# Second layer of a two-layer vision network: the recurrence's product gets an SBUF tile of its own, and a later input stands between product and sum

## The chip, the cores and the metric

The kernel runs on one core of one Trainium2 chip. The metric is the device time of one execution in microseconds (us). The version before the change has a median of 8306.25 us over three runs (8298.19 to 8308.66).

## What is computed

The network has two layers on an image batch of 16 x 128 x 56 x 56 in float32. The first layer (routed window attention with a feed-forward part) is not touched by the change. The second layer is a 3x3 convolution, whose output is read as many short sequences of 8 tokens with 16 channels, each of which goes through a small selective state-space model (32 inner channels, 16 states each), followed by a group normalisation and a residual sum. What matters here is the recurrence over the 8 tokens:

```
dA = jnp.exp(dt[..., None] * A)
dBx = dt[..., None] * Bm[:, :, None, :] * xc[..., None]
def step(h, inp):
    a, b, c = inp
    h = a * h + b
    return (h, jnp.sum(h * c[:, None, :], axis=-1))
```

Each token multiplies the state by its decay `a`, adds the input `b`, and weighs the new state with `c`.

## The kernel before, in words

**Layout.** The two layers run one after the other. The second one (function `layer1`) works through 16 images x 7 blocks = 112 groups. A group is 448 sequences in the free dimension. For one token its state has 32 x 16 = 512 values for each sequence, held as an SBUF tile `h` of 128 x 4 x 448; a token is done in two halves (`jp` 0 and 1) of 128 x 2 x 448 = 128 x 896 elements, so that 7 tokens to be advanced in two halves make 14 steps `k` of a group.

**What one token needs.** TensorE spreads the step sizes times the decay rates into a PSUM tile `a` (`decay`, L973; two buffers), and ScalarE takes the exponential in place (`decay_exp`, L976). TensorE spreads the inputs into a PSUM tile `x` (`spread`, L984; one buffer), and VectorE multiplies it with the token's row of `B` (tile `bb`, brought by DMA) into the SBUF tile `h`: this is the token's input (`inject`, L991). VectorE then makes the product of decay and previous state, in place in PSUM (`advance`, L1001), and adds it to the input (`complete`, L1006). The last token (l = 7) leaves out the sum: its product goes straight to `h` (L999), since its input reaches the output by another way (`product`, `direct`, `direct_mul`). GpSimd multiplies the whole state of a token, 128 x 1792 elements, with the token's row of `C` (`weigh`, L1010), and TensorE sums over the states (`gather`, L1019). `collect` (L1032) adds the direct part, tile `ud`; `gated` (L1035) is on GpSimd.

**Order of work.** The order on each engine is written out by hand in the loop at the end of `layer1`, and `_chain` keeps every engine to it; each engine works through its own queue in that order. At step k of a group VectorE gets `advance` of step k, what `work` puts in its list (`collect`, statistics), `complete` of step k, and `inject` for step k + 4; at k = 0 the list (`direct_mul`) comes after the `inject`. TensorE then gets `decay` for step k + 2 and `spread` for step k + 5, and ScalarE the exponential. At every odd k GpSimd gets `weigh` for the token just finished, and then the list of the step. GpSimd's queue in a group is therefore: weigh 1 (k = 1), in some groups a part of the store (k = 2, L1126), weigh 2 (k = 3), the second `gated` of the previous group (k = 4), weigh 3 (k = 5), four operations of `rate_sum` for the next group (k = 6, L922 to L925), weigh 4 (k = 7), four more (k = 8), weigh 5 (k = 9), `product` (k = 10, L951), weigh 6 (k = 11), weigh 7 (k = 13), the first `gated`.

**Buffers.** `h` has four buffers, given out in the order of the code: tokens 0 to 6 when their input is made, token 7 when its product is made. So the `inject` at k = 12, for token 1 of the next group, takes the buffer of token 5, which is free when weigh 5 is done; the one at the next k = 0 takes that of token 6 and waits for weigh 6. `w1` to `w4` are SBUF pools with one to four buffers for each tag.

The first layer has one line that matters as a comparison: `position` (L303), a multiply-add on VectorE that reads two SBUF tensors, runs beside the GpSimd operations of `beside` (L313 and L315), which work on other tiles.

The loop that sets the order:

```
if now:
    advance(*state_step(i, k))
for part in dve if k else ():
    part()
if now:
    complete(*state_step(i, k))
if inputs:
    inject(*inputs)
```

Of the kernel before, what the change touches and what calls it, by code (L numbers as in the profile page):

```python
# [10 lines left out]
F32 = mybir.dt.float32  # L11
U32 = mybir.dt.uint32
AF = mybir.ActivationFunctionType
ALU = mybir.AluOpType
# [3 lines left out]
P = 128  # L18
# [5 lines left out]
BLK = 448  # L24
# [771 lines left out]
def layer1(ctx: ExitStack, tc: tile.TileContext, x1, t, out, conv):  # L796
# [15 lines left out]
    nc = tc.nc  # L812
# [3 lines left out]
    cst = ctx.enter_context(tc.tile_pool(name="l1c", bufs=1))  # L816
    w1 = ctx.enter_context(tc.tile_pool(name="l1w1", bufs=1))
    w2 = ctx.enter_context(tc.tile_pool(name="l1w2", bufs=2))
# [14 lines left out]
    vec = conv.vec  # L833
# [5 lines left out]


    for w, name in ((wx, "b_kx"), (wv, "b_dtw")):
        k = w1.tile(list(w.shape), F32, tag="fold", name=name)
        nc.sync.dma_start(k, t[name])
        nc.vector.tensor_mul(w, w, k)
    nc.scalar.activation(adec, adec, AF.Exp)
    nc.vector.scalar_tensor_tensor(adec, adec, -1.0, mask, ALU.mult, ALU.mult)
    dd = cst.tile([P, P], F32, tag="dd", name="dd")
    nc.vector.tensor_scalar_mul(dd, ident, d_w)
    eps = cst.tile([P, 1], F32, tag="eps1", name="eps1")
    nc.vector.memset(eps, GN_EPS)  # L850
    neg = cst.tile([P, 1], F32, tag="neg", name="neg")
    nc.vector.memset(neg, -1.0)

    y, tails = conv.y, conv.tails
    pq = [ps_q.tile([P, 512], F32, tag=f"q{k}", name=f"pq{k}") for k in range(2)]
# [11 lines left out]
    def own(jp):  # L867
        return slice(2 * jp, 2 * jp + 2)
# [86 lines left out]
        nc.tensor.matmul(pq[0][:, 0:BLK], lhsT=cbm, rhs=p["cb"], start=True, stop=True)  # L955

    def direct_mul(p):
        ud = p["ud"] = w2.tile([P, 2, BLK], F32, tag="ud", name=f"ud_{p['n']}")
        for h in range(2):
            nc.vector.scalar_tensor_tensor(  # L960
                ud[:, h, :], pq[0][:, 0:BLK], vec[:, 6 + h : 7 + h], p["dtx"][:, h, :], ALU.mult, ALU.mult
            )


# [3 lines left out]
    def decay(p, l, jp):  # L968
        h, l4 = divmod(l, 4)
        a = p["a", l, jp] = ps_a.tile([P, 2, 512], F32, tag="a", name=f"a_{p['n']}_{l}_{jp}")[:, :, 0:BLK]  # L970
        for k in range(2):
            rows = slice(32 * (2 * jp + k), 32 * (2 * jp + k) + 32)
            nc.tensor.matmul(a[:, k, :], lhsT=adec[rows, l4, :], rhs=p["dt"][rows, h, :], start=True, stop=True)  # L973

    def decay_exp(p, l, jp):
        nc.scalar.activation(p["a", l, jp], p["a", l, jp], AF.Exp)  # L976

    def spread(p, l, jp):

        h, l4 = divmod(l, 4)  # L980
        x = ps_x.tile([P, 2, 512], F32, tag="x", name=f"x_{p['n']}_{l}_{jp}")[:, :, 0:BLK]
        for k in range(2):
            rows = slice(32 * (2 * jp + k), 32 * (2 * jp + k) + 32)
            nc.tensor.matmul(x[:, k, :], lhsT=mask[rows, l4, :], rhs=p["dtx"][rows, h, :], start=True, stop=True)  # L984
        px["x"] = x

    def inject(p, l, jp):
        if jp == 0:
            p["h", l] = w4.tile([P, 4, BLK], F32, tag="h", name=f"h_{p['n']}_{l}")
        weight = p["gate", 0, l].unsqueeze(1).to_broadcast([P, 2, BLK])  # L990
        nc.vector.tensor_mul(p["h", l][:, own(jp), :], px["x"], weight)  # L991

    def advance(p, l, jp):

        a, before = p["a", l, jp], p["h", l - 1][:, own(jp), :]
        if l == 7:
            if jp == 0:
                p["h", l] = w4.tile([P, 4, BLK], F32, tag="h", name=f"h_{p['n']}_{l}")
            nc.vector.tensor_mul(p["h", l][:, own(jp), :], a, before)  # L999
        else:  # L1000
            nc.vector.tensor_mul(a, a, before)  # L1001

    def complete(p, l, jp):
        if l < 7:
            h = p["h", l][:, own(jp), :]
            nc.vector.tensor_add(h, p["a", l, jp], h)  # L1006

    def weigh(p, l):
        c = p["c", l] = w4.tile([P, 4, BLK], F32, tag="cst", name=f"cst_{p['n']}_{l}")
        nc.gpsimd.tensor_mul(c, p["h", l], p["gate", 1, l].unsqueeze(1).to_broadcast([P, 4, BLK]))  # L1010
# [18 lines left out]
    def collect(p, h):  # L1029
        if h == 0:  # L1030
            p["ym"] = w1.tile([P, 2, BLK], F32, tag="ym", name=f"ym_{p['n']}")
        nc.vector.tensor_add(p["ym"][:, h, :], pq[1][:, 0:BLK], p["ud"][:, h, :])  # L1032

    def gated(p, h):
        nc.gpsimd.tensor_mul(p["ym"][:, h, :], p["ym"][:, h, :], p["zs"][:, h, :])  # L1035
# [117 lines left out]
    def work(i, k):  # L1153
# [8 lines left out]
        if prev:  # L1162
            if k == 0:
                pe += [partial(gather, prev, 5), partial(gather, prev, 6)]
            if k == 1:
                pe.append(partial(gather, prev, 7))
            if k == 3:
                dve.append(partial(collect, prev, 1))
            if k == 4:
                pool.append(partial(gated, prev, 1))  # L1170
            if k in (5, 6):
                pe.append(partial(project_out, prev, k - 5))
            b = prev["b"]
            if prev["g"] % 2 and k in (9, 10):
                dve.append(partial(statistics, b, prev["g"] - 10 + k))
            if prev["g"] == NBLK - 1:
                if k == 9:
                    dve.append(partial(statistics, b, NBLK - 1))
                if k == 12 and b < NB - 1:
                    residual(b, 0)  # L1180
# [26 lines left out]
        if p:  # L1207
            if i == len(groups) - 1 and k in (4, 6):
                residual(p["b"], k // 2 - 2)
            if k == 0:  # L1210
                dve.append(partial(direct_mul, p))
            if k == 7:
                pe.append(partial(skip, p, 0))
            if k in (8, 9, 10):
                pe.append(partial(gather, p, k - 7))
            if k == 12:
                dve.append(partial(collect, p, 0))
            if k == 13:
                if nxt:
                    pe.append(partial(direct, nxt))  # L1220
                pe += [partial(skip, p, 1), partial(gather, p, 4)]
                pool.append(partial(gated, p, 0))
            if k in (2, 6):
                bring(p, 0, {2: (4, 5), 6: (6,)}[k])
            if k in (1, 5, 9):
                bring(p, 1, {1: (3, 4), 5: (5, 6), 9: (7,)}[k])
# [41 lines left out]
    def state_step(i, k):  # L1268

        i, k = i + k // 14, k % 14  # L1270
        return (groups[i], 1 + k // 2, k % 2) if i < len(groups) else None

    def input_step(i, k):
        i, k = i + k // 14, k % 14
        return (groups[i], k // 2, k % 2) if i < len(groups) else None
# [8 lines left out]
    for i in range(-2, len(groups) + 3):  # L1284
        for k in range(14):
            now = 0 <= i < len(groups)
            pe, dve, pool = work(i, k)
            inputs = input_step(i, k + 4) if now or (i == -1 and k >= 10) else None
            further = input_step(i, k + 5) if now or (i == -1 and k >= 9) else None
            decays = state_step(i, k + 2) if now or (i == -1 and k >= 12) else None  # L1290

            if now:
                advance(*state_step(i, k))
            for part in dve if k else ():
                part()
            if now:
                complete(*state_step(i, k))
            if inputs:
                inject(*inputs)
            for part in () if k else dve:  # L1300
                part()
            if decays:
                decay(*decays)
            if further:
                spread(*further)
            if decays:
                decay_exp(*decays)
            if now and k % 2:
                weigh(groups[i], 1 + k // 2)
            for part in pe + pool:  # L1310
                part()
# [3 lines left out]
@with_exitstack  # L1315
def network(ctx: ExitStack, tc: tile.TileContext, t, out):
    NB = out.shape[0]
    dram = ctx.enter_context(tc.tile_pool(name="dram", bufs=1, space=bass.MemoryType.DRAM))
    x1 = [dram.tile([P, HW], F32, tag=f"x1_{b}", name=f"x1_{b}") for b in range(NB)]
    conv = Convolution(tc.nc, ctx.enter_context(tc.tile_pool(name="conv", bufs=1)), t, x1)  # L1320
    layer0(tc, t["x"], t, x1, conv)
    layer1(tc, x1, t, out, conv)
# [27 lines left out]
```

## Time and profile before

| what | value |
| --- | --- |
| median of the runs (lowest, highest) | 8306.25 us (8298.19, 8308.66) |
| time of the profiled execution, its span | 8305.77 us, 8304.0 us |
| first and last start of a `weigh` (L1010), 784 in all | 3205.9 us, 8277.0 us |
| busy in the span: PE, VectorE, ScalarE, GpSimd | 94%, 93%, 68%, 85% |
| `inject` L991 | 1568 x 1083 ns |
| `advance` L1001 (tokens 1 to 6), L999 (token 7) | 1344 x 1091 ns, 224 x 1084 ns |
| `complete` L1006 | 1344 x 1089 ns |
| `weigh` L1010 | 784 x 4000 ns |
| `rate_sum` on GpSimd, one of four operations | 1137 to 1145 ns |

The page gives times in us or, for one instruction, in ns. DVE is VectorE, ACT is ScalarE, POOL is GpSimd, PE is TensorE and PEld its weight load. A group line names the line of the code, the engine, the operation, and the tiles as out<-in, then the shapes and how often it ran; after the bar stand the total busy time in us and the mean of one in ns, and after the second bar the idle time of the engine ahead of it. A timeline line begins with start and duration in us. An instruction's duration is all the time from its start to its end on the engine, so time in which it is held up inside counts as busy.

### The profile page before, as it was taken

How to read it: one execution, taken by the hardware profiler on the slowest of the kernel's cores; microseconds unless marked ns; L12 is line 12 of the kernel's file. 1: busy time of each engine (PE TensorE's matmuls, PEld its weight loads, DVE VectorE, ACT ScalarE, POOL GpSimd, SP SyncE). 2: the span in 40 equal slices, each digit the busy share in tenths (PEclk: the TensorE clock that was granted, in tenths of full speed). 3: DMA queues.
4: the chain of work that ended last, by engine and by line, in shares of the span. 5: the costliest groups of instructions: out<-in, count | busy, mean ns of one | idle time of the engine just before them, and what ended most of it. 6: DMA issues, size and time to landing. Idle time of an engine off the chain costs nothing.

```text
span 8304.0 us, 151471 instructions
## 1 busy us (share of the span) xinstructions
PE 7835.1 (94%) x52860; PEld 3329.9 (40%) x52860; DVE 7736.9 (93%) x10346; ACT 5642.6 (68%) x10579; POOL 7054.9 (85%) x5692
## 2 busy tenths in 40 slices
PE   5999999999999998999999999999999999999998
PEld 3444444444444453333333333333333333333332
DVE  7999999999999976999999999999999999999998
ACT  4777777777777755666666666666666666666665
POOL 7888788888888725899989999999999989999997
PEclk8999999999999999999999999999999999999998
DMA  3333333333333323333333334334333343334333
GB/s 65 87 86 87 85 89 87 87 87 87 87 87 87 81 79 82 87 93 102 99 92 99 96 91 105 91 97 106 83 104 100 88 105 103 86 99 108 85 93 88
DMA packets 764584, 757.87 MB, mean 91 GB/s; under 512 B 188720, under 2 KB 663984, under 8 KB 761904
## 3 DMA queue, kind: packets, MB, share of 16 engines
q1 hardware_dynamic: 763824, 748.18, 34.9%
q8 instruction: 423, 6.93, 0.4%
q14 instruction: 337, 2.76, 0.1%
HBM read 439.61 MB, written 102.76 MB: 65 GB/s over the span
## 4 chain that ended last, share of the span: by engine, by line
PE 34%; DVE 24%; POOL 24%; issue 9%; ACT 9%; DMA 1%; SPq 0%; POOLq 0%; ACTq 0%; DVEq 0%
PE a L973 7%; DVE h L991 6%; DVE a L1001 5%; POOL cst L1010 5%; PE x L984 5%; POOL xh L315 5%; PE pq L1019 5%; PE pq L892 4%; POOL e L431 4%; DVE h L1006 4%; DVE lepe L512 3%; POOL tap L313 3%; POOL dtx L925 2%; PE pq L931 2%; DVE sst L415 2%
## 5 line engine op out<-in xcount | busy, mean ns | idle before, releaser
L1010 POOL TENSOR_TENSOR cst<-h,cb 128x1792 f32<-128x1792 f32 x784 | 3130.6, 4000 | 348.9 <-DVE h L1006 291.1
L976 ACT ACTIVATE a<-a 128x896 f32<-128x896 f32 x1568 | 1415.7, 903 | 1080.2 <-PE x L984 588.0
L991 DVE TENSOR_TENSOR h<-x,bb 128x896 f32<-128x896 f32 x1568 | 1697.5, 1083 | 96.6 <-PE x L984 58.2
L512 DVE SCALAR_TENSOR_TENSOR lepe<-vpad,lep,lepe 128x448 f32<-128x448 f32 x2688 | 1718.0, 678 | 0.5
L984 PE MATMUL x<-dtx,amask 32*128 32x448 f32 x6272 | 1626.4, 595 | 49.0 <-DVE h L991 38.5
L973 PE MATMUL a<-dt,adec 32*128 32x448 f32 x6272 | 1620.2, 593 | 53.7 <-DVE h L1006 49.9
L1006 DVE TENSOR_TENSOR h<-a,h 128x896 f32<-128x896 f32 x1344 | 1463.1, 1089 | 38.1
L1001 DVE TENSOR_TENSOR a<-a,h 128x896 f32<-128x896 f32 x1344 | 1465.7, 1091 | 26.7 <-ACT a L976 25.8
L431 POOL TENSOR_SCALAR e<-e,sst,zero 128x256 f32<-128x256 f32 x1568 | 861.1, 559 | 466.6 <-DVE sst L427 417.4
L421 ACT ACTIVATE e<-ps,sst 128x256 f32<-128x256 f32 x1568 | 728.6, 469 | 522.5 <-DVE sst L415 470.5
L973 PEld LDWEIGHTS a<-dt,adec 32*128 32x128 f32 x6272 | 474.5, 185 | 1066.5 <-DVE h L1006 501.4
L315 POOL TENSOR_TENSOR xh<-xh,tap 128x448 f32<-128x448 f32 x749 | 859.6, 1148 | 43.7
L184 PE MATMUL pq<-pad,conv 128*128 128x448 f32 x1890 | 834.8, 559 | 0.0
L1019 PE MATMUL pq<-cst,sel 128*32 128x448 f32 x6272 | 734.5, 553 | 0.8 <-POOL cst L1010 0.8
L415 DVE TENSOR_REDUCE sst<-ps 128x2 f32<-128x512 f32 x784 | 540.3, 689 | 107.9 <-PE ps L409 83.0
L146 ACT ACT_TABLE_LOAD x484 | 621.0, 1283 | 9.3 <-PEq L1341 0.7
L453 PE MATMUL ptt<-ident,e 128*128 128x128 f32 x3136 | 538.6, 283 | 93.5 <-POOL e L431 76.8
L984 PEld LDWEIGHTS x<-dtx,amask 32*128 32x128 f32 x6272 | 476.7, 185 | 365.9 <-DVE h L991 344.3
L409 PE MATMUL ps<-sel,q 32*64 32x256 f32 x6272 | 537.3, 411 | 53.2 <-ACT e L421 46.9
L313 POOL TENSOR_SCALAR tap<-pad,pos,zero 128x448 f32<-128x448 f32 x749 | 546.5, 730 | 35.7
L453 PEld LDWEIGHTS ptt<-ident,e 128*128 128x128 f32 x3136 | 366.6, 141 | 417.5 <-POOL e L431 237.0
L459 ACT COPY att<-ptt 128x512 f32<-128x512 f32 x784 | 458.7, 585 | 72.0 <-PE ptt L453 64.1
(175 smaller groups left out, 12040.7 us busy)
## 6 DMA issues: line engine op xcount, KB each, us to landing
sel<-kv SPq DMA_DIRECT2D x3136, 64.0 KB
bb<-db SPq DMA_DIRECT2D x336, 448.0 KB
cb<-dc SPq DMA_DIRECT2D x336, 448.0 KB
pad<-x SPq DMA_DIRECT2D x32, 784.0 KB
x<-r SPq DMA_DIRECT2D x112, 224.0 KB
pad<-x SPq DMA_DIRECT2D x16, 1568.0 KB
db<-bs SPq DMA_DIRECT2D x112, 224.0 KB
dc<-cs SPq DMA_DIRECT2D x112, 224.0 KB
```

The source lines that it names most:

```text
L315: nc.gpsimd.tensor_add(im["xh"][i], im["xh"][i], held["tap"])
L431: nc.gpsimd.tensor_scalar(e, e, im["st", w][:, 2, p : p + 1], zero, ALU.mult, ALU.add)
L453: nc.tensor.transpose(ptt[:, P * (2 * p + h) : P * (2 * p + h + 1)], e[:, h * P : (h + 1) * P], ident)
L512: nc.vector.scalar_tensor_tensor(out, src, lep[:, k : k + 1], acc, ALU.mult, ALU.add)
L973: nc.tensor.matmul(a[:, k, :], lhsT=adec[rows, l4, :], rhs=p["dt"][rows, h, :], start=True, stop=True)
L976: nc.scalar.activation(p["a", l, jp], p["a", l, jp], AF.Exp)
L984: nc.tensor.matmul(x[:, k, :], lhsT=mask[rows, l4, :], rhs=p["dtx"][rows, h, :], start=True, stop=True)
L991: nc.vector.tensor_mul(p["h", l][:, own(jp), :], px["x"], weight)
L1001: nc.vector.tensor_mul(a, a, before)
L1006: nc.vector.tensor_add(h, p["a", l, jp], h)
L1010: nc.gpsimd.tensor_mul(c, p["h", l], p["gate", 1, l].unsqueeze(1).to_broadcast([P, 4, BLK]))
L1019: nc.tensor.matmul(py[32 * j : 32 * j + 32], lhsT=sel[:, l4, :], rhs=p["c", l][:, j, :], start=False, stop=(l % 4 == 3), skip_group_check= ...
```

## The change

Three things change in `layer1`. The product of decay and state is no longer written back to PSUM over the decay, but to a new SBUF tile `m` with one buffer (128 x 2 x 448); the sum reads it from there. On VectorE the input of step k + 4 now stands between the product and the sum of step k. And the SBUF room is rearranged: the fold at the start uses the tag of `m`, two constants share a tile, and `ud` becomes two tiles, with one buffer for the first half and two for the second.

```diff
-        k = w1.tile(list(w.shape), F32, tag="fold", name=name)
+        k = w1.tile(list(w.shape), F32, tag="m", name=name)
...
-    eps = cst.tile([P, 1], F32, tag="eps1", name="eps1")
+    small = cst.tile([P, 2], F32, tag="small", name="small")
+    eps, neg = small[:, 0:1], small[:, 1:2]
     nc.vector.memset(eps, GN_EPS)
-    neg = cst.tile([P, 1], F32, tag="neg", name="neg")
...
     def direct_mul(p):
-        ud = p["ud"] = w2.tile([P, 2, BLK], F32, tag="ud", name=f"ud_{p['n']}")
         for h in range(2):
+            ud = p["ud", h] = (w1, w2)[h].tile([P, BLK], F32, tag=f"ud{h}", name=f"ud{h}_{p['n']}")
             nc.vector.scalar_tensor_tensor(
-                ud[:, h, :], pq[0][:, 0:BLK], vec[:, 6 + h : 7 + h], p["dtx"][:, h, :], ALU.mult, ALU.mult
+                ud, pq[0][:, 0:BLK], vec[:, 6 + h : 7 + h], p["dtx"][:, h, :], ALU.mult, ALU.mult
             )
...
         else:
-            nc.vector.tensor_mul(a, a, before)
+            m = p["m", l, jp] = w1.tile([P, 2, BLK], F32, tag="m", name=f"m_{p['n']}_{l}_{jp}")
+            nc.vector.tensor_mul(m, a, before)
 
     def complete(p, l, jp):
         if l < 7:
             h = p["h", l][:, own(jp), :]
-            nc.vector.tensor_add(h, p["a", l, jp], h)
+            nc.vector.tensor_add(h, p["m", l, jp], h)
...
-        nc.vector.tensor_add(p["ym"][:, h, :], pq[1][:, 0:BLK], p["ud"][:, h, :])
+        nc.vector.tensor_add(p["ym"][:, h, :], pq[1][:, 0:BLK], p["ud", h])
...
             for part in dve if k else ():
                 part()
-            if now:
-                complete(*state_step(i, k))
             if inputs:
                 inject(*inputs)
             for part in () if k else dve:
                 part()
+            if now:
+                complete(*state_step(i, k))
```

## The prediction

> **What bounds the kernel now.** I read the page's busy shares first, then the busy times of the second layer's stretch, then the timelines of VectorE and GpSimd in one group, and last the one VectorE line that already reads two SBUF tensors. The columns of the stretch are its length, then busy time (count) of PE, PEld, DVE, ACT and POOL.
>
> ```profile
> 3210.00:8270.00 5060.00, 4941.84 (x25823) 1812.67 (x25824) 4917.66 (x5034) 3392.98 (x4739) 4593.98 (x2152) 0.99 0.36 96
> ```
>
> VectorE is busy 4918 of 5060 us and GpSimd 4594 (91%): neither has room. The 784 weighs start between 3205.9 and 8277.0 us, so a group of seven takes 5071.1 / 783 x 7 = 45.33 us, and 112 groups are the layer. VectorE's timeline (start, duration) shows how it spends them:
>
> ```profile
> 6023.34 1.09 DVE L1006 TENSOR_TENSOR h<-a,h 128x896 f32<-128x896 f32 x1
> 6024.34 1.08 DVE L991 TENSOR_TENSOR h<-x,bb 128x896 f32<-128x896 f32 x1
> 6025.34 1.09 DVE L1001 TENSOR_TENSOR a<-a,h 128x896 f32<-128x896 f32 x1
> 6026.46 1.09 DVE L1006 TENSOR_TENSOR h<-a,h 128x896 f32<-128x896 f32 x1
> 6027.47 1.08 DVE L991 TENSOR_TENSOR h<-x,bb 128x896 f32<-128x896 f32 x1
> ```
>
> Starts are 1.00 us apart, but 1.12 from a product to its own sum: a dependence on the instruction just ahead costs 0.12. A step is 3.13 us. Every one of these operations has one operand in PSUM. TensorE is also nearly full and waits for VectorE (501 us for the sum), so the two are close together. GpSimd in the same stretch:
>
> ```profile
> 6027.78 4.00 POOL L1010 TENSOR_TENSOR cst<-h,cb 128x1792 f32<-128x1792 f32 x1 [1.22 <-DVE h L1006]
> 6032.07 1.14 POOL L922 TENSOR_TENSOR u<-u,e 128x448 f32<-128x448 f32 x1 [0.29 <-ACT u L916]
> 6033.29 1.14 POOL L923 TENSOR_TENSOR ln<-ln,u 128x448 f32<-128x448 f32 x1
> 6034.51 1.14 POOL L924 TENSOR_TENSOR dt<-dt,ln 128x448 f32<-128x448 f32 x1
> 6035.73 1.14 POOL L925 TENSOR_TENSOR dtx<-dt,xc 128x448 f32<-128x448 f32 x1
> 6036.82 4.01 POOL L1010 TENSOR_TENSOR cst<-h,cb 128x1792 f32<-128x1792 f32 x1
> ```
>
> A weigh lasts 4.00 us, a rate_sum operation 1.14 (1.22 apart).
>
> After the change the sum reads `m` and `h`, both in SBUF. The first layer has such an operation, L303. It takes 668/680/1439 ns (least, median, most), so something can double it. Two places of the timeline tell what:
>
> ```profile
> 235.67 1.14 POOL L315 TENSOR_TENSOR xh<-xh,tap 128x448 f32<-128x448 f32 x1
> 235.95 1.33 DVE L303 SCALAR_TENSOR_TENSOR xh<-pad,pos,xh 128x448 f32<-128x448 f32 x1
> ```
>
> ```profile
> 112.87 0.67 DVE L303 SCALAR_TENSOR_TENSOR xh<-pad,pos,xh 128x448 f32<-128x448 f32 x1
> 112.89 1.24 POOL L313 TENSOR_SCALAR tap<-pad,pos,zero 128x448 f32<-128x448 f32 x1
> ```
>
> In the first, GpSimd was there first and ended at 236.81; VectorE ended 0.48 later, about the time 448 elements take: it stood still until GpSimd had finished. In the second, VectorE was first and kept its 0.67, and GpSimd took 1.24 in place of its median 0.72. So whoever comes first holds the other off. When both have a queue they alternate, as GpSimd's operations beside a run of L303 show:
>
> ```profile
> 30.45 1.38 POOL L315 TENSOR_TENSOR xh<-xh,tap 128x448 f32<-128x448 f32 x1
> 31.93 0.97 POOL L313 TENSOR_SCALAR tap<-pad,pos,zero 128x448 f32<-128x448 f32 x1
> 32.98 1.38 POOL L315 TENSOR_TENSOR xh<-xh,tap 128x448 f32<-128x448 f32 x1
> 34.35 1.09 POOL L297 TENSOR_SCALAR xh<-pad,pos,vec 128x448 f32<-128x448 f32 x1
> ```
>
> Each is 0.24 to 0.37 longer than alone (0.72 and 1.14), while L303 averages 6.98 / 6 = 1.16 us there; even L297, which starts with no gap, lets VectorE in first.
>
> [...] L1006, which reads PSUM beside the weighs, never exceeds 1.093 us. [...] L1142, two SBUF inputs of 784 with GpSimd idle, took 0.975[...]. So the sum alone keeps its 1.09. [...]
>
> **Part by part.**
>
> Removed: 0.12 us where a sum follows its product directly, in 10 of 12 sums of a group (collect or statistics stand between in the others), 112 x 10 x 0.124 = 139 us at most. `m` has one buffer, so the next product must now wait for the sum just ahead of it. No VectorE row shows that wait alone. GpSimd's does: L313 starts 0.10 after L315 has read its one-buffer `tap`, L297 starts 0.01 before L315's end. I take 0.12 (the two cancel), with 0 as the other end.
>
> Moved: the sum behind an inject, so a weigh is ready 1.0 us later, and step 0's sum also behind two direct_muls, 1.2 more. Behind L991 stand its own waits for `x`, `bb` and the buffer of `h` (96.6 us in all now). No DMA moves and only VectorE's queue is reordered. PSUM's `a` is free after the product, not the sum; that helps TensorE, which has slack if VectorE gets slower.
>
> At nothing: the product's target (L999 writes SBUF in 1.084, L1001 PSUM in 1.091); the fold (its last read is at 3166 us, the first product at 3198); the constants; the two `ud` tiles (the first is read at step 12 before it is rewritten at the next step 0, the second keeps two buffers). Without that cover a reused `ud` would cost at most its 0.68 a group.
>
> Added: the hold. The bounds for one sum are 0 and a weigh's 4.0; the nearest row (L303) gives the rest of GpSimd's instruction. I walk one group's queues. Rules: a held sum ends 0.95 after GpSimd's instruction (0.48 for 448 elements plus 0.475, the difference of L1006 and L1032); the next VectorE operation starts 0.08 before that; GpSimd's next ends at the sum's end plus its own length less 0.14 (33.37 to 34.36 for a 1.14 one); unhindered ones follow with 0.05 overlap; a weigh starts 0.2 after its sum.
>
> Weigh 3 starts at 0; sum 6 is already held, ends 4.95. Rate_sum 1 and 2 end 5.95 and 7.17; sum 7, ready at 6.87, is held by the second and ends 8.12. Rate_sum 3 and 4 end 9.12 and 10.34; sum 8, ready at 10.04, ends 11.29. Weigh 4 ends 15.15; sum 9 16.10. In the second rate_sum the same happens: operations end 17.10, 18.32, 20.27, 21.49, sums 10 and 11 19.27 and 22.44. Weigh 5 ends 26.30, product 27.39, weigh 6 31.34, weigh 7 35.29. Token 7 has no sums, but inject at step 12 waits for weigh 5 (ready 23.9, starts 26.5) and at step 0 for weigh 6 (30.7 to 31.55). After two direct_muls sum 0 is held by weigh 7, ends 36.24. Product and inject follow, and sum 1 ends 39.25; weigh 1 runs 39.45 to 43.45. Sum 2, held, ends 44.40; product, collect, inject, sum 3 end 47.94; weigh 2 runs 48.14 to 52.14; sum 4 ends 53.09, sum 5 56.09; weigh 3 starts at 56.29. Where the reuse wait of `m` lies open (before products 1, 3 and 5) it adds 0.37.
>
> A group is 56.66 us, 11.33 more: 112 x 11.33 = 1269. On the profiled execution's 8305.8 (span 8304.0 and 1.8 around it; 0.4 under the median) that is 9575.
>
> **Rivals.** *Sharing in pieces*: a long weigh might give way element by element[...]. L303 speaks against it, but no row shows a 4 us instruction. [...] *No run-ahead*: if no sum slips in beside the next token's (GpSimd keeps its turn between rate_sums), each of six tokens takes weigh 4.00, held sum 0.87, product and inject 2.12, sum 1.09, start 0.2 = 8.28; with collect 0.53, rate_sum 2 x 2.3 more, weigh 7 3.95 and product 1.1 a group is 59.9: 9940. *No hold, the other side*: [...] Then the sum is 1.09, the 139 us decide, and it is 8167 if reuse of `m` costs nothing; at 0.12 it is 8306. The point is a mean sum of 1.09 + 139/1344 = 1.19 us; above it the kernel is slower. The order is fixed by the chain, so the change does happen.
>
> **How the numbers follow.** Hold as walked 0.70 (own range 9420 to 9750, a microsecond either way for what the walk leaves out of TensorE and ScalarE), sharing 0.14, no run-ahead 0.08, no hold and faster 0.05, no hold and within 0.2% 0.03. 0.2% is about what a measurement can tell from no change. The range 9280 to 9800 leaves out the last three.
>
> **What would show it.** The sum's mean: near 1.95 us (five of 12 at 2.5 to 3.3, four near 1.25, three at 1.09), busy 2620 us in all. Weighs behind a sum near 4.8, others 4.0. L991 waiting for the weigh some 3.4 us a group, 380 in all, where it is 18.4. Product to inject to sum 1.00 apart; sum to next product 1.12. If the sum stays at 1.09, I am wrong on the hold; at 2.0 with every weigh stretched alike, it is sharing.

## The result and the profile after

The kernel after takes 9776.62 us (median of 4 runs, 9773.81 to 9777.91) against 8303.99 us before: 1472.6 us more, ratio 1.1773 (95% interval 1.1753 to 1.1794). Its profiled execution took 9773.81 us, with a span of 9772.0. The second layer's stretch, columns as before (length, then busy time of PE, PEld, DVE, ACT, POOL, and the granted clock of TensorE):

```profile
3210.00:9730.00 6520.00, 5800.48 (x25792) 2055.41 (x25794) 5851.98 (x5026) 3400.60 (x4734) 5281.06 (x2151) 0.87 0.29 74
```

No engine is full any more: VectorE 90%, GpSimd 81%, and a part of both is time spent standing still inside an instruction. TensorE's busy time grew from 4942 to 5800 us for the same work, while its granted clock fell from 0.99 to 0.87. The 784 weighs start from 3203.0 to 9744.5 us, so a group takes 6541.5 / 783 x 7 = 58.48 us where it took 45.33. Three groups of the page carry the difference:

```profile
L1011 POOL TENSOR_TENSOR cst<-h,cb 128x1792 f32<-128x1792 f32 x784 | 3266.3, 4172 | 1207.7 <-PE x L984 885.5
L1007 DVE TENSOR_TENSOR h<-m,h 128x896 f32<-128x896 f32 x1344 | 2408.9, 1792 | 0.0
L991 DVE TENSOR_TENSOR h<-x,bb 128x896 f32<-128x896 f32 x1568 | 1695.8, 1082 | 564.6 <-issue 213.7
```

The sum's mean went from 1089 to 1792 ns, 12 x 0.703 = 8.44 us a group. The idle time ahead of the inject went from 96.6 to 564.6 us, 4.18 a group; that ahead of the product from 26.7 to 132.5, 0.94 a group; that ahead of the sum, 38.1, is gone, 0.34. Together 13.22, where the group grew by 13.15. About two thirds are held sums and about one third late inputs.

VectorE's timeline where a weigh is running, and GpSimd's of the same time:

```profile
6027.39 1.08 DVE L991 TENSOR_TENSOR h<-x,bb 128x896 f32<-128x896 f32 x1
6028.39 3.05 DVE L1007 TENSOR_TENSOR h<-m,h 128x896 f32<-128x896 f32 x1
6031.54 1.09 DVE L1002 TENSOR_TENSOR m<-a,h 128x896 f32<-128x896 f32 x1
6032.55 1.08 DVE L991 TENSOR_TENSOR h<-x,bb 128x896 f32<-128x896 f32 x1
6033.55 1.08 DVE L1007 TENSOR_TENSOR h<-m,h 128x896 f32<-128x896 f32 x1
```

```profile
6026.51 3.98 POOL L1011 TENSOR_TENSOR cst<-h,cb 128x1792 f32<-128x1792 f32 x1 [2.43 <-PE x L984]
6030.45 1.99 POOL L922 TENSOR_TENSOR u<-u,e 128x448 f32<-128x448 f32 x1
6032.51 1.13 POOL L923 TENSOR_TENSOR ln<-ln,u 128x448 f32<-128x448 f32 x1
6033.72 1.91 POOL L924 TENSOR_TENSOR dt<-dt,ln 128x448 f32<-128x448 f32 x1
6035.71 1.14 POOL L925 TENSOR_TENSOR dtx<-dt,xc 128x448 f32<-128x448 f32 x1
6036.80 4.87 POOL L1011 TENSOR_TENSOR cst<-h,cb 128x1792 f32<-128x1792 f32 x1
```

The weigh ends at 6030.49, the sum 0.95 us later at 6031.44: it had started 2.1 us before the weigh's end and did its work after it. The rate_sum operation that was next takes 1.99 instead of 1.14, since it in turn stood behind the sum. The weigh itself is unharmed (3.98) unless a sum is ahead of it (4.87).

### The profile page after: what moved, and what is told of

Read it like the earlier page. It is cut to its first block, busy times and chain, and to the rows that moved or that the text cites. A ratio compares the mean times of both kernels' runs of the same rounds, so it can differ in the third digit from the quotient of the medians.

```text
span 9772.0 us, 153035 instructions
## 1 busy us (share of the span) xinstructions
PE 8701.8 (89%) x52860; PEld 3577.3 (37%) x52860; DVE 8683.6 (89%) x10346; ACT 5654.0 (58%) x10579; POOL 7736.2 (79%) x5692
## 5 line engine op out<-in xcount | busy, mean ns | idle before, releaser
L1011 POOL TENSOR_TENSOR cst<-h,cb 128x1792 f32<-128x1792 f32 x784 | 3266.3, 4172 | 1207.7 <-PE x L984 885.5
L1007 DVE TENSOR_TENSOR h<-m,h 128x896 f32<-128x896 f32 x1344 | 2408.9, 1792 | 0.0
L973 PE MATMUL a<-dt,adec 32*128 32x448 f32 x6272 | 1788.5, 649 | 469.3 <-DVE m L1002 301.6
L991 DVE TENSOR_TENSOR h<-x,bb 128x896 f32<-128x896 f32 x1568 | 1695.8, 1082 | 564.6 <-issue 213.7
L984 PE MATMUL x<-dtx,amask 32*128 32x448 f32 x6272 | 1857.3, 672 | 212.7 <-DVE h L991 198.0
L1002 DVE TENSOR_TENSOR m<-a,h 128x896 f32<-128x896 f32 x1344 | 1466.2, 1091 | 132.5 <-ACT a L976 1.8
L973 PEld LDWEIGHTS a<-dt,adec 32*128 32x128 f32 x6272 | 523.1, 204 | 1640.4 <-DVE m L1002 896.5
L984 PEld LDWEIGHTS x<-dtx,amask 32*128 32x128 f32 x6272 | 544.7, 211 | 734.3 <-DVE h L991 707.0
L922 POOL TENSOR_TENSOR u<-u,e 128x448 f32<-128x448 f32 x224 | 443.3, 1979 | 72.8 <-ACT u L916 72.8
```

Of the source, the lines that this page charges most:

```text
L1002: nc.vector.tensor_mul(m, a, before)
L1007: nc.vector.tensor_add(h, p["m", l, jp], h)
```

## The experiments

The times in the text are medians; each run of experiments has its own median of the kernel before (8307.5 to 8308.3 us).

**1. The order alone, and the tile alone.** The first is the kernel before with this:

```diff
-            if now:
-                complete(*state_step(i, k))
             if inputs:
                 inject(*inputs)
             for part in () if k else dve:
                 part()
+            if now:
+                complete(*state_step(i, k))
```

> The kernel before with the new order alone: the product stays in PSUM, in place over the decay, and the sum of step k comes after the inject of step k + 4. Hold theory: no sum reads two SBUF tensors, so L1006 keeps 1.09 us and nothing is held; the 0.12 us between a product and its sum goes, 139 us at most, so 8170 to 8306 us, the upper end if TensorE takes over as the bound. Rival, that the loss comes from the sum being later and every weigh starting later: about 9700 us.

Measured: 8562.5 us, ratio 1.0305 (1.0288 to 1.0323); the sum has 1081 ns. So the order makes no hold, and it isn't most of the loss, but it costs 254 us where I had expected none or a gain. TensorE's list of groups in this run says why:

```profile
L973 PE MATMUL a<-dt,adec 32*128 32x448 f32 x6272 | 1623.1, 594 | 746.4 <-DVE h L1006 744.5
```

With the product in PSUM the decay for step k + 2 needs the buffer that the sum of step k still reads; the sum is now one operation later, TensorE waits 744.5 us for it (49.9 before), and the spread that stands behind that decay in TensorE's queue makes the next inject wait: 424.4 us of idle time ahead of L991 against 96.6.

The second is the kernel after with the old order put back:

```diff
+            if now:
+                complete(*state_step(i, k))
             if inputs:
                 inject(*inputs)
             for part in () if k else dve:
                 part()
-            if now:
-                complete(*state_step(i, k))
```

> The kernel after with the old order: the product goes to the SBUF tile m, and the sum follows it directly, ahead of the inject. Hold theory: the sum reads two SBUF tensors, is held by the weigh as before, and between two sums stand the same two operations, so 9600 to 9900 us with a mean sum of 1.8 to 2.1 us. Rival, that the order makes the loss: near 8306 us.

Measured: 9649.0 us, ratio 1.1613 (1.1594 to 1.1633), mean sum 1981 ns. The tile alone makes 1341 us of loss, the order alone 254, both 1473. The two parts belong together in one respect: with the tile, the decay waits for the product and no longer for the sum (in the kernel after, 301.6 us of TensorE's idle time ahead of L973 end with the product, none with the sum).

**2. The length of the hold.** In the kernel after each weigh becomes two instructions:

```diff
-        nc.gpsimd.tensor_mul(c, p["h", l], p["gate", 1, l].unsqueeze(1).to_broadcast([P, 4, BLK]))
+        for s in (slice(0, 2), slice(2, 4)):
+            nc.gpsimd.tensor_mul(
+                c[:, s, :], p["h", l][:, s, :], p["gate", 1, l].unsqueeze(1).to_broadcast([P, 2, BLK])
+            )
```

> The kernel after with each weigh as two instructions of 128x896 instead of one of 128x1792; the same work on GpSimd. Hold theory (whole instructions hold each other): a sum that comes early in a weigh gets in at the boundary in the middle, after 2 us instead of 4, so the longest holds halve to about 2 us over the sum's own and a group falls from 58.5 to about 51 us: 8950 us, between 8750 and 9200. Rival, sharing element by element (the reads add up, however cut): unchanged, 9750 to 9850 us.

Measured: 9285.1 us, ratio 1.1177 (1.1158 to 1.1196): 491 us less than after, where sharing would have changed nothing, though less than I had put (at most 9200 us). The mean sum is 1405 ns, the longest 2879 in place of 4625. The control is the kernel before with the same cut.

> The kernel before with each weigh as two instructions of 128x896, the control for the halves in the kernel after (9285, 491 us under it). If those 491 us are shorter holds, the cut does little where nothing is held: 8230 to 8340 us. If they come from the first half of a weigh starting a sum earlier, or from the cut itself, the kernel before gains several hundred us too: 8000 us or less.

Measured: 8375.8 us, ratio 1.0082 (1.0066 to 1.0099). There the cut costs 68 us, a little more than I had allowed, so it is no gain in itself: the hold goes by whole instructions, and a shorter GpSimd instruction holds for a shorter time. In the kernel after with the halves, too, a held sum ended 0.95 us after GpSimd's instruction (6024.39 and 6023.44).

**3. Which sums are held.** Only one half of each token uses the SBUF tile; the other half's product stays in PSUM. For the first halves:

```diff
-            m = p["m", l, jp] = w1.tile([P, 2, BLK], F32, tag="m", name=f"m_{p['n']}_{l}_{jp}")
+            m = p["m", l, jp] = a
+            if jp == 0:
+                m = p["m", l, jp] = w1.tile([P, 2, BLK], F32, tag="m", name=f"m_{p['n']}_{l}_{jp}")
```

> The kernel after, but only the products of the first halves (jp 0, even steps) go to the SBUF tile m; those of the second halves stay in PSUM, in place. Hold theory: in the kernel after it is the even sums that are held by the rest of a weigh (2.2 to 3.05 us at steps 2, 4 and 6, while the odd sums there take 1.08), so nearly the whole loss stays: 9400 to 9750 us. Rival, that every sum with two SBUF inputs costs about the same: half the loss, near 9040 us.

Measured: 9727.9 us, ratio 1.1712 (1.1692 to 1.1731). Six two-input sums a group cost nearly as much as twelve, because each is held longer. The groups by form:

```profile
L1009 DVE TENSOR_TENSOR h<-m,h 128x896 f32<-128x896 f32 x672 | 1826.3, 2718 | 0.0
...
L1009 DVE TENSOR_TENSOR h<-a,h 128x896 f32<-128x896 f32 x672 | 723.0, 1076 | 0.0
```

The same line in the same kernel: 1076 ns with one operand in PSUM, 2718 with both in SBUF. The mirror, with `jp == 1`:

> The mirror of the last: only the products of the second halves (jp 1, odd steps) go to m. Hold theory: five VectorE operations lie between a weigh's start and the next odd sum, over 5 us, and a weigh takes 4, so an odd sum comes when the weigh is over, and only rate_sum holds some: 8500 to 8800 us, little above the order alone (8563). Rival, every such sum costs about the same: near 9040 us.

Measured: 9172.3 us, ratio 1.1040 (1.1022 to 1.1059): far better than the first halves, but above my 8500 to 8800. The odd sums at steps 1, 3 and 5 average 1.08, 1.28 and 1.12 us, as the theory has it. What I missed is step 11, where they average 3.98: rate_sum has put weigh 5 late, so it starts when that sum is about to. The group's end is late too, as in the kernel after: 2.55 us of idle time ahead of the inject at step 0.

```profile
5997.47 3.97 POOL L1013 TENSOR_TENSOR cst<-h,cb 128x1792 f32<-128x1792 f32 x1
...
5998.05 4.33 DVE L1009 TENSOR_TENSOR h<-m,h 128x896 f32<-128x896 f32 x1
```

Again 0.94 us from the weigh's end (6001.44) to the sum's (6002.38). Neither theory of equal cost for each sum nor mine for this half held; where GpSimd's instruction starts is what counts.

**4. No reading on GpSimd.** The weigh is replaced, in the kernel after and in the one before, by

```diff
-        nc.gpsimd.tensor_mul(c, p["h", l], p["gate", 1, l].unsqueeze(1).to_broadcast([P, 4, BLK]))
+        nc.gpsimd.memset(c, 0.0)
```

> The kernel after with the weigh left out: GpSimd fills cst with zeros in its place (it writes SBUF and reads none; the states' part of the output is missing). Hold theory: the weighs hold no sum any more, only rate_sum, gated, product and store do; mean sum 1.1 to 1.35 us; a step is 1.00 + 1.00 + 1.19 (the wait for the one buffer of m, 1.19 from sum to next product) = 3.19 us where before had 3.13, so 50 to 250 us above the kernel before with the same memset, 8300 to 8550 us. Rival, that the loss comes from the order and the buffers alone: near 9700 us. Third, that order and tile win once nothing is held: 100 us or more below the kernel before with the memset.

> The kernel before with the weigh left out in the same way (GpSimd fills cst with zeros; the states' part of the output is missing); the comparison for the last. VectorE bounds a group with 3.13 us a step and GpSimd's waits go: 8200 to 8310 us in all theories.

Measured: 8682.3 us for after, 8243.0 for before. The mean sum is 1157 ns. A sum that starts inside the fill isn't held:

```profile
6021.92 1.59 POOL L1011 MEMSET cst<- 128x1792 f32 x1
6022.35 1.08 DVE L1007 TENSOR_TENSOR h<-m,h 128x896 f32<-128x896 f32 x1
```

It begins 0.43 us after the fill and takes its bare time, 1.08 us, ending 0.08 us before the fill does. So the weighs' reading makes 1473 - 439 = 1034 us of the loss, with the limit that the fill is also shorter than a weigh (1.59 us). The other 439 us are far more than the 50 to 250 I had put: even without the weighs, order and tile lose. Per group that is 3.92 us: 0.82 in the sums (12 x (1157 - 1088) ns, where rate_sum's operations still meet sums: L924 averages 1809 ns, against 1135 in the kernel before with the fill), 2.36 in the idle time ahead of the inject (315.2 us against 50.9), and 0.62 more ahead of product and sum together (132.8 us against 25.5 and 38.3), where the wait for the one buffer of `m` has taken the place of the old one.

Most of the 2.36, 2.05 us, stands at step 0, and it goes with the granted clock of TensorE. From weigh 7 to the next weigh 1 the kernel after with the fill takes 11.20 us on average and the one before with the fill 9.45, which is 196 of the 439 us. In the 24 groups in which TensorE has its full clock during the products of `inner` at step 12 (the input tile `xc` of a later group) the former takes 9.47 us too; in the 38 in which it has half of it, 12.59.

**5. The group's end.** The stretch from weigh 7 to the next weigh 1 was 10.1 us in the kernel after. I moved TensorE's products of `inner` for `xc` (two in the code, four instructions in the trace) by one step:

```diff
-            if k == 12:
+            if k == 13:
                 eighth.insert(0, partial(inner, far, "xc", wx, w3, c1_b))
```

> The kernel after with the four products of inner for tile xc (TensorE, with ScalarE's table load) put at step 13 instead of step 12 of TensorE's list. Theory: the stretch from weigh 7 to the next weigh 1 is 10.1 us instead of the 8.2 of the walk because the inject at step 12, held by weigh 5, lets TensorE's spread for step 13 go late and these products stand between it and the next spread; moved, 0.5 to 1.9 us a group come back, 9570 to 9720 us. Rival, that the stretch is long for another reason (the holds themselves): 9760 to 9800 us.

Measured: 9955.8 us, slower still (1.1985, 1.1965 to 1.2005), with 11.64 us from weigh 7 to weigh 1. The wait that I meant did shrink: the idle time ahead of the inject fell from 564.6 to 391.3 us, at step 0 from 2.54 to 1.02 us a group. But `direct` stands behind the moved products, and direct_mul now waits for it ahead of the sum. VectorE and TensorE in that run:

```profile
6022.02 1.09 DVE L991 TENSOR_TENSOR h<-x,bb 128x896 f32<-128x896 f32 x1 [1.02 <-issue]
6026.33 1.28 DVE L960 SCALAR_TENSOR_TENSOR ud<-pq,vec,dtx 128x448 f32<-128x448 f32 x2 [3.22 <-PE pq L955]
```

```profile
6021.85 3.36 PE L892 MATMUL pq<-seq,wx 128*128 128x448 f32 x4
6024.99 1.30 PE L955 MATMUL pq<-cs,cbm 128*128 128x448 f32 x2
```

Next, the kernel after with the sum ahead of the inject at step 0 alone:

```diff
+            if now and k == 0:
+                complete(*state_step(i, k))
             if inputs:
                 inject(*inputs)
             for part in () if k else dve:
                 part()
-            if now:
+            if now and k:
                 complete(*state_step(i, k))
```

> The kernel after with the old order at step 0 of each group alone. Theory: the inject at step 0 waited 2.56 us in the kernel after and 0.15 in the tile-only run, and weigh 7 to weigh 1 took 10.09 us there and 9.03 here: with the sum first about 1.1 us a group comes back, 9560 to 9720 us, near the tile alone (9649). Rival, the holds alone make the group's end: 9760 to 9790 us.

Measured: 9785.5 us (1.1781, 1.1762 to 1.1801), no gain: my theory fell. The inject of step 0 follows the sum without idle time (in the timeline at 6018.16), but the sum at step 0 now comes early in weigh 7 and is held by it (3.75 us on average, 1.14 in the kernel after), and inject and direct_mul, which used that time, come after it. Weigh 7 to weigh 1 is 10.08 us again. The late input and the held sum each fill the time that the other would.

**6. Towards a faster kernel.** Two runs without the tile, product in PSUM: the order alone with the last diff (old order at step 0), and the same with TensorE's spread ahead of its decay:

```diff
-            if decays:
-                decay(*decays)
             if further:
                 spread(*further)
+            if decays:
+                decay(*decays)
```

> The order alone (product in PSUM), but with the old order at step 0 of each group, sum ahead of inject. Theory: the order costs mainly at the group's end, where the inject of step 0 comes one operation sooner than TensorE, busy with the products of inner at step 12, can have its x ready (weigh 7 to weigh 1 grew by 2.28 us in the order-only run): 8310 to 8480 us. Rival, the order costs in every step (the decay held back until the later sum): 8520 to 8563 us.

> The order alone (product in PSUM) with two amendments: at step 0 of a group the sum stays ahead of the inject, and TensorE does spread ahead of decay, so that the inject's x no longer waits behind a decay that waits for the late sum. Theory: the order alone was slow (8563) since the injects wait for x; with both amendments the 0.12 us between product and sum is won in most steps: 8170 to 8300 us, a little faster than before. Rival, TensorE has no slack and bounds the layer: 8306 us or more.

Measured: 8461.0 (1.0186, 1.0169 to 1.0203) and 8503.9 us (1.0239, 1.0222 to 1.0257). Step 0 accounts for 102 of the order's 254 us; the larger part is lost in the other steps, where the rival had put all of it. Spread first didn't help: the product then waits for the exponential (146.2 us ahead of L1001, 26.7 before) and the injects still wait, 141.6 us of it put down to TensorE's L973. No version here that computes the whole layer beats the kernel before. Two buffers for `m` weren't tried; they would take 3.5 KB more of SBUF in each partition.

## Why the prediction was right, and where it was short

Forecast 9575, measured 9776.6, inside 9280 to 9800 but above the 9420 to 9750 that I gave the hold as walked: of the 1473 us the forecast had 1269.

**The hold** was the right mechanism with the right rules. A held sum ended 0.95 us after GpSimd's instruction, and the next GpSimd instruction then ended later by what was left of the sum (1.99 us in place of 1.14 in the timeline above); the median sum, at 1082 ns, had its bare time. The mean sum is 1.79 us against 1.95 forecast. Sum by sum the agreement is partly luck: the walk's times make about 2.5 us of sum 0, 2.9 of sum 9 and 1.25 of sum 11, and they took 1.14, 2.30 and 2.26. Sharing in pieces is ruled out by the 3.05 us line above, a sum that began 2.1 us ahead of the weigh's end and still ended 0.95 us after it, and by the halves. No run-ahead is ruled out too: at 6033.55 a sum got in between two rate_sum operations, and the second of them took 1.91 us.

**The walk**, in distances between the starts of weighs (forecast from its text without the 0.37 for reuse; measured as means over the groups of the trace; before for comparison):

| from weigh | 1 to 2 | 2 to 3 | 3 to 4 | 4 to 5 | 5 to 6 | 6 to 7 | 7 to 1 |
| --- | --- | --- | --- | --- | --- | --- | --- |
| before | 6.59 | 6.31 | 9.40 | 8.72 | 5.05 | 3.96 | 5.29 |
| forecast | 8.69 | 8.15 | 10.29 | 11.15 | 5.90 | 3.95 | 8.16 |
| after | 8.82 | 8.33 | 10.28 | 11.13 | 5.92 | 3.93 | 10.09 |

Six of seven are right to 0.2 us, and the 0.31 that the first two are over stands against the 0.37 for reuse. The term that was mis-sized is the last: 1.93 us a group, 216 us in all, more than the whole shortfall of 202.

**The failed step** is the inject at step 0, "for weigh 6 (30.7 to 31.55)": I gave it 0.85 us of waiting for a buffer, and it waited 2.54 on average, for TensorE. VectorE and TensorE at one group's end in the kernel after:

```profile
6057.34 1.09 DVE L991 TENSOR_TENSOR h<-x,bb 128x896 f32<-128x896 f32 x1 [0.97 <-PE x L984]
6058.35 1.08 DVE L1002 TENSOR_TENSOR m<-a,h 128x896 f32<-128x896 f32 x1
6062.54 1.09 DVE L991 TENSOR_TENSOR h<-x,bb 128x896 f32<-128x896 f32 x1 [3.11 <-POOL cst L1011]
```

```profile
6053.91 1.86 PE L973 MATMUL a<-dt,adec 32*128 32x448 f32 x4 [3.08 <-DVE h L999]
6055.43 1.86 PE L984 MATMUL x<-dtx,amask 32*128 32x448 f32 x4
6057.23 3.35 PE L892 MATMUL pq<-seq,wx 128*128 128x448 f32 x4
...
6060.52 1.12 PE L984 MATMUL x<-dtx,amask 32*128 32x448 f32 x2
...
6061.43 0.95 PE L984 MATMUL x<-dtx,amask 32*128 32x448 f32 x2
```

The second inject is put down to a weigh that had ended 0.8 us earlier; the spread for it ended at 6062.38, 0.16 us ahead of it. TensorE had stood still behind the held sums, then did decay, spread and inner's four products, and only then the spread that this inject needs. I had counted on TensorE having slack once VectorE gets slower; but the new order also makes the inject of step 0 come one operation sooner, while `x` has one buffer, and TensorE did all this at half its clock (0.50 granted), which the walk left out. Its stretch of `inner`'s products (columns as before, the granted clock third from the end), and below it the same products and the inject of step 0 behind them in the run with the order alone, where the clock was 1.00:

```profile
6057.23:6060.58 3.35, 3.35 (x10) 1.24 (x8) 2.09 (x2) 1.42 (x2) 3.35 (x2) 0.50 0.43 113
```

```profile
6000.49 1.77 PE L892 MATMUL pq<-seq,wx 128*128 128x448 f32 x4
```

```profile
6003.37 1.09 DVE L991 TENSOR_TENSOR h<-x,bb 128x896 f32<-128x896 f32 x1 [0.67 <-POOL cst L1010]
```

Six runs have this order on both engines. Their groups (111 in each), sorted by the granted clock during `inner`'s products at step 12, with the mean idle time ahead of the inject at step 0 (groups in which the clock changed meanwhile are left out):

| run | at full clock | at half clock |
| --- | --- | --- |
| order alone | 0.67 us (107 groups) | 2.84 us (3 groups) |
| tile for first halves | 0.68 us (107 groups) | 2.52 us (2 groups) |
| tile for second halves | 0.67 us (2 groups) | 2.96 us (67 groups) |
| kernel after with the fill | 0.62 us (24 groups) | 2.93 us (38 groups) |
| weighs in halves | no group | 2.82 us (69 groups) |
| kernel after | no group | 2.77 us (76 groups) |

So my 0.85 would have done for a TensorE at full clock, even with held sums (first halves). The table sorts groups and doesn't set the clock; and what the 1.93 us would be at full clock isn't shown, since the kernel after has no such group and an earlier inject would let the sum at step 0 run into weigh 7, as the walk had it.

The moved `inner` shows that these products are what the inject waits for; the run with the old order at step 0 shows that taking this wait away by that order alone brings nothing, since weigh 7 then holds the sum. So the walk needed TensorE's queue as a third one, at the clock that TensorE has there, and the two costs don't add.

**The reuse of `m`** was rightly seen and too small: sum to next product is 1.19 us, not 1.12, start to start; in the run with the tile for second halves alone, where `m` isn't written again at once, it is 1.00. Product to inject is 1.01: the old 0.12 is gone. In a step the order wins 0.12 and the one buffer takes 0.19, which by itself is a loss.

**The idle time ahead of the inject** was forecast at 380 us for the weigh; it is 207 for the weigh and 565 in all. At step 12, where the walk had 2.6 us for weigh 5, it is 1.29 us; at step 13, where the walk had none, 0.97.

**The rival on the other side** (8167, or 8306 with the reuse) was priced wrongly. Its condition, no hold by the weigh, can be seen in the pair with the fill, and there the change costs 439 us, not -139 to 0. It left out TensorE, its clock and the input's single buffer.

## What to carry over

Before a VectorE operand is moved from PSUM to SBUF, look whether the instruction then reads two SBUF tensors while GpSimd runs long reading instructions: here such a sum ended 0.95 us after GpSimd's, and a queue walk of both engines gave the cost well, to 0.2 us in six of seven stretches. Put every queue into that walk that feeds the moved step, TensorE's too, and look at TensorE's granted clock, which here was 0.99 before and 0.87 after. A dependence that is taken from between two neighbours can come back as the wait for a single buffer between two others (in a step here, 0.12 us won and 0.19 lost).

## What I had not expected of the hardware

In the kernel after, TensorE was often at half its clock when it had stood still. The four decay matmuls behind an idle stretch of 3.08 us (above, at 6053.91) took 1.86 us as a group, and so did the next four; the granted clock from 6052.3 to 6062.3 was 0.50. Behind 2.08 us of waiting another such group took 1.02 us, at a granted clock of 1.00:

```profile
6015.52 1.02 PE L973 MATMUL a<-dt,adec 32*128 32x448 f32 x4 [2.08 <-DVE m L1002]
```

Of the 94 stretches of 2.5 us and more in which TensorE stood still in the second layer of the kernel after, 80 saw the clock fall to half before work went on or within 0.5 us of it; of the 143 between 0.5 and 1.5 us it was 7. Standing still that long isn't the only way, though: in the kernel after with the fill the clock fell 101 times, with only one stretch above 1.5 us. What else makes it fall stays open.

The stretches at half clock in the second layer of the kernel after, 231 in all, last 3.41 us (32 of them) or a multiple of it (152 last 6.83 us). In the group shown above the clock fell at 6052.2, 1.3 us after TensorE's last matmul, and came back at 6062.4, after 8.5 us of work without a pause. How much of the 1.93 us at the group's end is this clock wasn't tested by a run of its own; the table above has what the groups show.
